# Graph attention and transformer on one core: side work placed by hand among the products, masks turned as pairs of bytes, merged preparation steps

## The chip, the cores and the metric

The kernel runs on one core of a Trainium2 chip. The metric is the device time of one execution in microseconds; of three runs the median is given. A profile of one execution shows what each engine does: TensorE (PE, with its weight loads PEld), VectorE (DVE), ScalarE (ACT), GpSimd (POOL), and SyncE (SP), from whose queue all DMAs are issued.

## What is computed

Two graph attention layers run one after the other on the same 4096 x 4096 adjacency matrix of int32, and a transformer layer follows. There are 8 heads of 32 features.

```python
def _gat_layer(x, adj_mat, W, a):
    Wh = jnp.einsum('nd,hdo->hno', x, W)
    src = jnp.einsum('hno,ho->hn', Wh, a[:, :O])
    dst = jnp.einsum('hno,ho->hn', Wh, a[:, O:])
    e = jax.nn.leaky_relu(src[:, :, None] + dst[:, None, :], LRELU_SLOPE)
    e = jnp.where(adj_mat[None, :, :] > 0, e, NEG_INF)
    alpha = jax.nn.softmax(e, axis=-1)
    out = jnp.einsum('hnm,hmo->hno', alpha, Wh)
    return jnp.transpose(out, (1, 0, 2)).reshape(N, -1)
...
h = jax.nn.elu(_gat_layer(x, adj_mat, W1, a1)) + x
out = jax.nn.elu(_gat_layer(h, adj_mat, W2, a2)) + h
...
qkv = layer_norm(x, g1, be1) @ w_qkv
scores = jnp.where(mask, jnp.einsum('nhd,mhd->hnm', q, k) * SCALE, -jnp.inf)
out = jnp.einsum('hnm,mhd->nhd', softmax(scores), v).reshape(n, DIM)
x = x + out @ w_proj + b_proj
x = x + jax.nn.gelu(layer_norm(x, g2, be2) @ w1 + b1) @ w2 + b2
```

## The kernel before, in words

**How a graph layer becomes products.** The leaky ReLU has two branches, and the exponential of a sum is a product of exponentials. So the weights of a row over its neighbours are a sum over those neighbours whose term passes a threshold (one branch) and over the others (the other branch). The threshold test depends on row and neighbour and gives a 0/1 byte; everything else is a factor of the row or of the neighbour. The layer is then a set of TensorE products whose stationary operand is a tile of 128 x 128 bytes of fp8 (the test ANDed with the mask, or the mask alone) and whose moving operand is `vst`, the neighbours' values multiplied by their exponentials, as two halves of fp16 that together carry an fp32 value.

**Tiling.** The rows are cut into blocks; `TILES` gives their sizes in tiles of 128 rows: 4, 4, 8, 8, 8 for the first layer and 8, 8, 8, 8 for the second. A *group* is one layer, one block, one pair of heads `p` (4 of them) and four key tiles `g` (8 of them). The main loop runs over all groups in that order. A group of an 8-tile block has 8 x 4 x 4 = 128 products, written at L1234 into six PSUM banks that stay open over the eight groups of a head pair. At the end of a pair, ACT copies the banks out (L1240, L1246), and `pair_end` puts four steps (load, sum, divide, out) on the list `later`, one of which is taken per group.

**What lies beside the products.**
- `compare` (L1008) makes the bytes for the group two ahead: four key tiles of two heads, on DVE (L1023) or ACT (L1021), and then one AND with the mask on DVE (L1026). It needs `s_b`, a row of terms spread over the partitions by DMA (`s_fetch`, L1000).
- Masks: `mask_loads` brings 128 rows x 1024 columns of the adjacency as int32 (512 KB); `mask_turn` clips them to bf16 (DVE, L844), turns them with eight transposes (TensorE, L849) into a bank of the pool "turn" (two buffers), and ACT copies the bank to fp8 (L850). Block 0 keeps its masks in SBUF; the others are written to DRAM and fetched again by `mask_fetch` when their block comes. There are 128 such units, all in the first layer. The table `turns` tells which units go beside which group; units of block 0 go beside the first head pair.
- Preparation of four key tiles (`features`, `term_rows`, `values`): rows of x are loaded and turned (fp32 transposes L916, copies L919); the terms' rows are a product with 8 output rows (L926), copied (L934) and written to DRAM; values and terms of each tile are two double products of 272 columns (L942), followed by the sign change (L950), the exponentials (ACT, L953, L961), the check reduction (L954), two scales (L962), the product (L963), the fp16 half (ACT, L971) and the rest (DVE, L972). Eight preparations make a layer.

**What sets the order.** Inside the graph layers the instructions of each engine are ordered by the tile framework's own scheduler. The preparations of both layers start only when their layer starts: three ahead of its first product, the rest in the gaps between the tiles of the first five groups. In the attention part, TensorE, ACT and DVE follow the order of the program (`manual_schedule`); SP works its queue in the order that it is given.

**The transformer.** For each of eight blocks of 512 rows: normalisation, queries and keys in two fp16 halves written to DRAM and stacked back (`stack`, L1387), values kept. Then attention over 512 units, and then the projection and feed-forward part. Before the first unit of attention the queries of block 0 and its first four mask chunks are loaded (`load_queries`, `load_chunk`, L1467); pools for these are opened after the QKV part has closed its own.

## Time and profile before

| | |
|---|---|
| median of 3 runs | 3524.44 us (3523.82 to 3525.63) |
| profiled execution | 3524.0 us, mean granted TensorE clock 0.982 |
| busy: TensorE | 3357.4 us |
| busy: DVE | 2903.2 us |
| busy: ACT | 2730.9 us |
| busy: GpSimd | 1239.1 us, none of it between 51 and 1783 us |
| last product of the graph layers | 1783.6 us |
| first product of attention | 1914.3 us |
| last product of attention | about 3226 us |

Busy times are averages over stages with different limits, so a reading begins by cutting the span where the order of work changes. In a table of stretches each row gives the stretch, its length, and for each engine the busy time and, in brackets, the count of instructions; then the mean granted TensorE clock, the busy share of the DMA engines and their rate. In a row of groups by line, the first number after the bar is the busy time of all instructions of that line, the second the mean of one in nanoseconds, and after the second bar stands the idle time of the engine just before them with what ended it. In a row of waits the three numbers are the total in microseconds, the number of waits and the longest.

### The profile page before, as it was taken

Reading aid. Unit: us, or ns where it says so; the run is one execution under the profiler, and the core shown is the slowest. Engines: PE = TensorE matmul, PEld = TensorE weight load, DVE = VectorE, ACT = ScalarE, POOL = GpSimd, SP = SyncE. Lnnn points to the kernel's source line nnn. Section 1 sums busy time; section 2 is a strip of 40 time slices with the busy share of each in tenths; the row PEclk is TensorE's granted clock in tenths of the full one; section 3 lists DMA queues with packets and bytes.
Section 4 is the critical chain, followed back from the end, with each engine's and each line's share of the span. In section 5 each row is a group of like instructions: output and inputs, shape, how many; then the busy total and the mean of one; then the engine's idle time right before and its main releaser. Section 6 shows DMA issues by size and latency. Waiting matters only on the chain.

```text
span 3524.0 us, 99099 instructions
## 1 busy us (share of the span) xinstructions
PE 3357.4 (95%) x43715; PEld 2128.8 (60%) x43715; DVE 2903.2 (82%) x3580; ACT 2730.9 (77%) x3528; POOL 1239.1 (35%) x538
## 2 busy tenths in 40 slices
PE   6898999999989999999987999999999999997998
PEld 4698999999969999999963111111111121112666
DVE  5898999999889999999944999999999999996111
ACT  4799999998778888888854777777777777775332
POOL 0000000000000000000001999999999999996110
PEclk8999999999999999999998999999999999998999
DMA  4357554441221312111156010101010110002110
GB/s 140 123 191 242 167 167 157 157 123 39 68 62 33 86 39 80 45 58 37 26 135 171 10 40 13 37 19 31 25 25 25 25 37 13 28 9 68 44 47 25
DMA packets 199560, 252.76 MB, mean 72 GB/s; under 512 B 88080, under 2 KB 134672, under 8 KB 199120
## 3 DMA queue, kind: packets, MB, share of 16 engines
q1 hardware_dynamic: 199120, 246.34, 23.3%
q8 instruction: 344, 5.64, 0.7%
q14 instruction: 96, 0.79, 0.1%
HBM read 203.83 MB, written 42.47 MB: 70 GB/s over the span
## 4 chain that ended last, share of the span: by engine, by line
PE 73%; DVE 11%; ACT 9%; DMA 3%; issue 2%; POOL 2%; SPq 0%; DVEq 0%; ACTq 0%; POOLq 0%
PE bank L1234 34%; PE u_ps L1480 12%; PE u_av L1494 11%; PE u_dn L1494 6%; ACT t L1021 5%; DVE u_e L1489 4%; PE misc L1666 3%; PE misc L1419 2%; POOL u_both L1580 2%; DVE t L1023 1%; ACT u_ps L1487 1%; ACT stage L850 1%; DVE t L1026 1%; PE misc L1650 1%; PE turn L926 1%
## 5 line engine op out<-in xcount | busy, mean ns | idle before, releaser
L1234 PE MATMUL bank<-vst,t 128*128 128x66 f16 (+1 forms) x24576 | 1517.9, 203 | 22.0 <-DVE t L1026 15.5
L1234 PEld LDWEIGHTS <-t 128*128 128x128 fp8e4 x24576 | 1505.6, 97 | 33.2 <-DVE t L1026 18.0
L1234 PE MATMUL bank<-vst,mask 128*128 128x132 f16 x8192 | 1503.5, 222 | 0.0
L1021 ACT ACTIVATE t<-s_b,g_negd 128x1024 int8<-128x1024 f32 (+1 forms) x1296 | 1260.0, 1063 | 88.8 <-PE bank L1234 88.1
L1489 DVE SCALAR_TENSOR_TENSOR u_e<-u_mask,u_ps 128x1024 f32<-128x1024 uint8 x1024 | 1201.7, 1215 | 100.7 <-ACT u_ps L1487 95.8
L1580 POOL TENSOR_TENSOR u_both<-u_e 128x1024 f32<-128x1024 f32 x512 | 1199.8, 2367 | 238.5 <-DVE u_e L1489 238.3
L1487 ACT ACTIVATE u_ps<-u_ps 128x1024 f32<-128x1024 f32 x1024 | 1010.8, 1008 | 296.2 <-PE u_ps L1480 277.2
L1234 PEld LDWEIGHTS <-mask 128*128 128x128 fp8e4 x8192 | 803.6, 98 | 1.9 <-issue 0.9
L1026 DVE TENSOR_TENSOR t<-t,mask 128x2048 int32<-128x2048 int32 (+1 forms) x288 | 590.6, 2051 | 119.5 <-ACT t L1021 109.8
L1023 DVE TENSOR_SCALAR t<-s_b,g_negd 128x1024 fp8e4<-128x1024 f32 (+1 forms) x1008 | 638.5, 687 | 2.7 <-PE bank L1234 2.3
masks.py:197 POOL MEMSET u_ident<- 128x128 f32 x1 | 0.2, 204 | 1785.7 <-DMA u_wq<-in_L_gnn_w_qkv_dram 1785.7
L1480 PE MATMUL u_ps<-u_q,u_k 128*128 128x512 f16 x2048 | 580.5, 384 | 36.8 <-DMA u_q<-half_d 21.7
L1480 PEld LDWEIGHTS <-u_k 128*128 128x128 f16 x2048 | 139.2, 97 | 743.7 <-issue 685.4
L1494 PE MATMUL u_av<-u_e,u_v 128*32 128x512 f32 x4096 | 547.1, 605 | 0.0
L1494 PE MATMUL u_dn<-u_both,u_ones 128*32 128x512 f32 x2048 | 274.0, 605 | 1.3 <-POOL u_both L1580 1.3
L1494 PEld LDWEIGHTS u_av<-u_e,u_v 128*32 128x32 f32 x4096 | 80.9, 108 | 219.1 <-issue 211.3
L1657 ACT ACTIVATE u_hid<-misc,u_b 128x512 f32<-128x512 f32 x64 | 42.3, 683 | 142.9 <-PE misc L1650 142.8
L850 ACT ACTIVATE stage<-turn 128x1024 fp8e4<-128x1024 bf16 x112 | 114.2, 1037 | 1.1 <-PE turn L849 1.0
L1673 DVE TENSOR_TENSOR u_xres<-u_xres,misc 128x256 f32<-128x256 f32 x32 | 13.5, 421 | 122.7 <-PE misc L1666 122.7
L1666 PE MATMUL misc<-u_w,u_hid 128*128 128x256 f32 x512 | 111.8, 379 | 0.0
L1650 PE MATMUL misc<-ln_cols,u_w 128*128 128x512 f32 x256 | 111.2, 592 | 0.0
L1494 PEld LDWEIGHTS u_dn<-u_both,u_ones 128*32 128x32 f32 x2048 | 40.6, 108 | 110.9 <-issue 108.4
(104 smaller groups left out, 1749.8 us busy)
## 6 DMA issues: line engine op xcount, KB each, us to landing
g_rows<-in_adj_dram SPq DMA_DIRECT2D x128, 512.0 KB
mask<-mask SPq DMA_DIRECT2D x120, 256.0 KB
s_b<-s_d SPq DMA_DIRECT2D x56, 512.0 KB
u_mask<-mask SPq DMA_DIRECT2D x32, 512.0 KB
mask<-stage SPq DMA_DIRECT2D x28, 512.0 KB
half_d<-u_halves SPq DMA_DIRECT2D x32, 256.0 KB
u_k<-half_d SPq DMA_DIRECT2D x32, 256.0 KB
u_q<-half_d SPq DMA_DIRECT2D x32, 256.0 KB
```

Of the source, the lines that this page charges most:

```text
L850: nc.scalar.activation(staged[0].rearrange("p i g n -> p (i g) n")[:, :, t * P : (t + 1) * P], pt, AF.Identity, saturate=False,)
L1021: nc.scalar.activation(to.bitcast(I8), s, AF.Sign, bias=negd, scale=-1.0)
L1023: nc.vector.tensor_scalar(to, s, negd, None, op0=ALU.is_ge, saturate=False)
L1026: nc.vector.tensor_tensor(both, both, mask.unsqueeze(1).to_broadcast(list(both.shape)), op=ALU.bitwise_and)
L1234: nc.tensor.matmul(to, left, right, start=k not in opened, stop=last)
L1480: nc.tensor.matmul(ps[:, j, :], k_st[:, h, mt * P : (mt + 1) * P], q_st[:, h, :], start=True, stop=True,)
L1487: nc.scalar.activation(ps, ps, AF.Exp, scale=SCALE)
L1489: nc.vector.scalar_tensor_tensor(e, mask, 0.0, ps, op0=ALU.not_equal, op1=ALU.mult)
L1494: nc.tensor.matmul(to[j * O : (j + 1) * O, :], lefts[j], es[j // 2][:, j % 2, :], start=start, stop=stop,)
L1580: nc.gpsimd.tensor_tensor(both, es_of[i - 1][u], es_of[i][u], op=ALU.add)
L1650: nc.tensor.matmul(ph, w1_sb[:, k, f * P : (f + 1) * P], hn[:, k, :], start=(k == 0), stop=(k == DC - 1),)
L1666: nc.tensor.matmul(po[:, :D], hid[:, f, at : at + P], w2_sb[:, f, :], start=(f == 0), stop=(f == FC - 1),)
```

## The change

1. **Blocks**: `TILES` of the first layer becomes 8, 8, 8, 8, so all groups have 128 products.
2. **Masks**: a unit is now 256 rows x 512 columns. `mask_clip` clips to fp8, with the bytes of two neighbouring rows side by side; the pair is read as one fp16 element, so `mask_turn` needs four transposes, and ACT copies 512 elements of 16 bits. Clips are placed one or two groups ahead of their transposes. A check at the start tests that four bit patterns survive a transpose.
3. **Preparation**: the weights carry a third set of 8 columns (the destination term times the slope), the sign, slope and the factor 32 are multiplied into the weights, so one exponential of 16 columns replaces two of 8; one copy takes both sets of terms; the fp16 rest is subtracted on GpSimd (`split`), a step later. The terms' rows come from one transpose of a 128 x 32 tile of the terms kept in SBUF, in place of the product with 8 output rows, and four small DMAs write them. The call of `check_values` is gone.
4. **Order**: TensorE, ACT and DVE follow the program's order in the whole of the graph layers. For each group a list `side` of steps with positions between 0 and 1 is made (preparation, compare, AND, mask turns, clips, pair-end steps), sorted, and given out between the tiles of the group's products.
5. **Change of layer**: the weights of the second layer are made during the first; six of its eight preparations stand beside the last six groups of the first layer, and two beside its own groups 3 and 4.
6. **QKV and attention**: the pools of queries and masks are opened before QKV; key stacks are issued one block later; the queries of block 0 and its four mask chunks are loaded during QKV. Normalisation pools are split (`u_ln`, `u_lnc`), the halves get three buffers.
7. **Feed-forward**: the projection weight's load is issued first, and two pools change places.

```diff
-TILES = ((4, 4, 8, 8, 8), (8, 8, 8, 8))
+TILES = ((8, 8, 8, 8), (8, 8, 8, 8))
...
-    mask_p = ctx.enter_context(tc.tile_pool(name="g_mask", bufs=11))
+    mask_p = ctx.enter_context(tc.tile_pool(name="g_mask", bufs=10))
...
+    def mask_clip(nb, c, i):
+
+        v = rows_p.tile([P, G * P, 2], F8, name="adj_8", bufs=6)
         nc.vector.tensor_scalar(
-            v.rearrange("p m s -> p (m s)"), r, 1.0, -(2.0**-30), op0=ALU.min, op1=ALU.max
-        )
...
+            v.rearrange("p m r -> p r m"),
+            loaded.pop((nb, c, i)),
+            1.0,
+            -(2.0**-30),
+            op0=ALU.min,
+            op1=ALU.max,
             saturate=False,
         )
+        clipped[nb, c, i] = v.rearrange("p m r -> p (m r)").bitcast(F16)
+        load_ahead(1)
...
+        pt = turn_bank([P, G, P], F16)
+        for m in range(G):
+            nc.tensor.transpose(pt[:, m, :], v[:, m * P : (m + 1) * P], ident_h)
+        to = built[nb, c][:, i // 2].bitcast(U16)
+        nc.scalar.activation(to[:, :, i % 2 * P : (i % 2 + 1) * P], pt.bitcast(U16), AF.Copy)
...
-        nc.vector.tensor_tensor(halves[:, :, 1, :], part, halves[:, :, 0, :], op=ALU.subtract)
+        def split(t):
+            part = held.pop(t).rearrange("p h i v -> p h (i v)")
+            halves = vst[q][:, t].rearrange("p h (k v) -> p h k v", k=2)
+            nc.scalar.copy(halves[:, :, 0, :], part)
+            nc.gpsimd.tensor_tensor(halves[:, :, 1, :], part, halves[:, :, 0, :], op=ALU.subtract)
...
+        def term_rows():
+
+            pr = bank()[: G * H, :P]
+            nc.tensor.transpose(
+                pr, L.terms[:, 0, G * q : G * (q + 1)].rearrange("p t h -> p (t h)"), ident_f
+            )
+            sr = some.tile([G * H, P], F32, name="g_sr")
+            nc.scalar.copy(sr, pr)
+            for t in range(G):
+                at = (G * q + t) * P
+                nc.sync.dma_start(s_d[l][:, at : at + P], sr[t * H : (t + 1) * H])
...
+    prepared = {i: (0, i + 2) for i in range(NG - 2)}
+    for l in range(1, NL):
+        start = l * len(TILES[0]) * per_block
+        for q in range(NG):
+            prepared[start + q + (-6 if q < NG - 2 else -3)] = (l, q)
...
+    ordered = {mybir.EngineType.PE, mybir.EngineType.Activation, mybir.EngineType.DVE}
+    ctx.enter_context(tc.manual_schedule(engines=ordered))
+    begin()
...
+        if made:
+            steps = preparation(*made, lambda: turn_bank([P, 512], F32))
+            beside(steps, 0.0, 0.9)
+        if i + 2 < len(groups):
+            steps = compare(i + 2)
+            beside(steps[:-1], 0.25 if made else 0.0, 0.95)
+            beside(steps[-1:], 0.96, 1.0)
+        beside([lambda u=u: mask_turn(*u) for u in turns.get(i, ())], 0.0, 0.9)
...
+            while side and (n == tiles - 1 or side[0][0] * tiles < n + 1):
+                side.pop(0)[1]()
...
-                    if i == 1:
-                        stack(k_st[:, :, cols], 1, (0, 0, 1, 1), cols)
...
+                for b in (nb - 1,) if nb + 1 < NNB else (nb - 1, nb):
+                    if b >= 0:
+                        at = slice(b * NB, (b + 1) * NB)
+                        stack(k_st[:, :, at], 1, (0, 0, 1, 1), at)
+                    if b == 0:
+                        load_queries(0)
+                if 2 <= nb < 2 + NT // MC:
+                    load_chunk(0, nb - 2)
```

## Prediction

> **What bounds the kernel now.** I read first the busy shares (TensorE 95% of the span), then cut the span where the order of the work changes and asked for the busy time of each engine in each stretch:
>
> ```profile
> core 0: us, PE busy (x) PEld busy (x) DVE busy (x) ACT busy (x) POOL busy (x), PEclk, DMA share, GB/s
> 0.00:51.20 51.20, 22.98 (x98) 13.10 (x98) 29.22 (x83) 23.12 (x55) 1.08 (x8) 0.92 0.54 156
> 51.20:155.50 104.30, 84.15 (x784) 60.58 (x785) 74.91 (x201) 67.25 (x166) 0.00 (x0) 0.88 0.37 118
> 155.50:368.60 213.10, 193.65 (x3973) 189.39 (x3971) 197.51 (x390) 210.64 (x342) 0.00 (x0) 0.98 0.65 211
> 368.60:961.30 592.70, 590.25 (x12786) 587.66 (x12787) 536.73 (x643) 546.31 (x648) 0.00 (x0) 1.00 0.39 122
> 961.30:1076.00 114.70, 101.93 (x1120) 74.28 (x1119) 103.94 (x249) 84.68 (x197) 0.00 (x0) 0.97 0.22 66
> 1076.00:1783.60 707.60, 707.57 (x15493) 705.70 (x15490) 637.49 (x734) 618.64 (x740) 0.00 (x0) 1.00 0.17 49
> 1783.60:1914.30 130.70, 94.16 (x322) 57.14 (x322) 49.41 (x103) 63.01 (x159) 0.61 (x2) 0.86 0.72 181
> ```
>
> The sixth stretch is the floor: 121 groups of 128 products (a group is four key tiles of one head pair in a block of 8 tiles) in 707.6 us, 5.85 us each, TensorE never idle; there DVE is busy 5.27 us and ACT 5.11 us a group. The graph layers hold 256 such groups, 1497 us, but end at 1783.6. The other 287 us lie in the other five stretches: 51 us before the first product; 81 over the floor in the first head pair of block 0 (512 products, 23.4 us worth); 50 in the rest of the two 4-tile blocks, where ACT is full (210.6 of 213.1); 31 in the blocks of 8 whose masks are turned beside them; 74 at the change of layer. A second look, at the waits between QKV and attention, shows one more hole, in which TensorE, then ACT and DVE behind it, wait for a load:
>
> ```profile
> PE u_ps L1480 <- DMA u_q<-half_d: 21.7, 1, 21.7
> ```
>
> Prices are from the groups by line:
>
> ```profile
> L850 ACT ACTIVATE stage<-turn 128x1024 fp8e4<-128x1024 bf16 x112 | 114.2, 1037 | 1.1 <-PE turn L849 1.0
> L844 DVE TENSOR_SCALAR adj_bf<-g_rows 128x1024 bf16<-128x1024 int32 x128 | 87.0, 685 | 3.6 <-DMA g_rows<-in_adj_dram 3.6
> L942 PE MATMUL turn<-g_w_ext,g_ft 128*128 128x272 f32 x256 | 71.9, 412 | 9.1 <-DVE g_prod L963 6.1 <-DVE g_negd L950 1.1 <-ACT g_rows L934 0.5
> L972 DVE TENSOR_TENSOR vst<-g_prod,vst 128x528 f16<-128x528 f32 x64 | 44.8, 700 | 0.5 <-ACT vst L971 0.3
> L963 DVE TENSOR_TENSOR g_prod<-turn,g_prod 128x512 f32<-128x512 f32 x64 | 43.9, 686 | 0.1
> L926 PE MATMUL turn<-g_ft,g_w_ext 128*8 128x512 f32 x64 | 37.0, 709 | 0.3 <-ACT g_ft L919 0.2
> ```
>
> The reader is to see 128 mask units of 1.04 us on ACT and 0.69 us on DVE, and a preparation that costs DVE more than TensorE.
>
> **What the Trainium skill says.** "Vector Engine (DVE) Microarchitecture Reference", section 5.1, lets a one-source operation with source and destination in SBUF and an even outermost dimension take two elements a cycle, whatever the type; two-tensor operations not. The trace agrees: the clip L844 takes 0.67 ns an element, the mask AND L1026 2.28 us for 2048. "TensorE: Matmul & The Clock Gate", Part 1, has 55.6 ns between products of 128 columns; here a group with eight transposes lasts 6.26 us against 5.84, 53 ns each. "SBUF — State Buffer", "Who interferes with whom": GpSimd shares a port pair with DVE's two-element mode and with the second input of DVE's two-tensor operations, and the later one waits out the whole instruction. No run here shows that: GpSimd is idle in the graph layers.
>
> **The change part by part.** All sums are against the profiled span, 3524.0 us (other runs 3523.8 to 3525.6).
>
> *Masks.* A unit keeps its 1024 elements a partition, but two rows become one 16-bit column: 4 transposes in place of 8, so TensorE 0.22 us in place of 0.44, and ACT copies 512 elements, priced as the 512-element copy L919, 0.59 us in place of 1.04. The DVE clip now writes single bytes two apart. If it keeps the two-element mode it stays at 0.64 us net (two in 1.29); if not, 1024 elements at the AND's 1.11 ns are 1.14 us. I take 0.64: the page's condition does not ask for step one. Both ends go into the range. Loads keep 512 KB, in pieces of 2 KB in place of 4; the 155.5 to 368.6 stretch moved 211 GB/s at 0.65 busy, and four loads plus writes in a 15 us group need some 190: I cost that at nothing, hidden behind DVE.
>
> *Blocks of 8 tiles throughout.* 64 half groups become 32 whole ones; the products stay 32,768. Comparing 1024 in place of 512 columns saves a fixed part only.
>
> *Preparation (16 times: 8 four-tile steps, two layers).* TensorE loses L926 (4 x 512 columns of fp32; 1.9 us in the timeline) for one small transpose, keeps 8 transposes (0.9) and 8 double-pass products, now 280 columns (3.8): 4.8 us in place of 6.6. DVE loses the subtraction L972 (to GpSimd) and one small scale, keeps copy, reduction, product, scale: 0.16 + 0.42 + 0.69 + 0.17, four times 1.44, less overlap 5.2 us. ACT loses one small exponential a tile and the 512-wide row copy. The end checks of a layer's values (L974) are no longer called: a few small reductions, hidden under TensorE, 0. GpSimd gets 528 elements a tile; by L1580 (2.37 us for 1024) an estimate of 1.2 us. Port waits cost DVE between 0 and 4.8 us a preparation; I take 2.0 in the first, 1.5 in the second layer.
>
> *Start.* Only layer 0's weights are made (DVE free near 11.5 us in place of 13.7), two preparations with eight clips take 2 x 7.8 + 5 for filling and ports (32), term rows to DRAM and back as before 6.5 (39), four compares on ACT and the AND 6.5: first product near 47. The second group's compare and four more clips follow on DVE: 5 carried over. 52.
>
> *Groups 0 to 5*, each with a preparation and four units. DVE: compares 2.3, AND 2.2, preparation 5.2, clips 2.6, ports 2.0 = 14.3; ACT 12.6; TensorE 5.85 + 4.8 + 0.9 = 11.5. Before, DVE-bound groups at the change of layer held DVE 91% busy; I take 15.2. Six are 91.
> *Groups 6 to 27*, 1.45 units each: TensorE 6.17, DVE 5.27 + 0.93 = 6.20, ACT 5.97. I take 6.25: 138.
> *Groups 28 to 91*, one unit each: TensorE 6.07, DVE 5.91, ACT 5.70. 64 x 6.08 = 389.
> *Groups 92 to 121*: 30 x 5.85 = 176.
> *Change of layer.* Six preparations beside groups 122 to 127, two beside 131 and 132. DVE 2.3 + 2.2 + 5.2 + 0.8 + 1.5 = 12.0, TensorE 10.65; I take 12.6: 76; then 3 x 6.3 + 2 x 12.6 = 44. The rows of the last block must be written by the last pair end, two steps a group, before step 6 reads them one group ahead: covered by a group of 6 us.
> *Groups 133 to 255*: 123 x 5.85 = 720.
> Sum 52 + 91 + 138 + 389 + 176 + 76 + 44 + 720 = 1686 against 1783.6: **-98**.
>
> *QKV and attention.* Queries and masks of block 0 are loaded inside QKV (3 MB more in about 100 us at 0.72 busy; TensorE has work there throughout), key stacks one block late, so SP no longer waits at each. Attention can start once the last banks are emptied, about 1895 in place of 1914.3; I take -17 of at most -20 and at least -10, since work buffers reuse space under the last stores. *Pools and the projection weight's earlier load*: the 11.9 us wait there is for the attention output, not the weight; 0, bounds -5 and +3. The pair end in fixed order delays the first normalisation of QKV by some 2 us: +1.
>
> Total 3524 - 98 - 17 + 1 = **3410**.
>
> **The rivals.**
> *A, as summed*: 3410, own range 3390 to 3430. Chance 0.55.
> *B, the byte-strided clip loses the two-element mode*: +0.5 us on 128 clips, on the path where DVE binds: start 4, six groups x 2.0 = 12, 22 x 0.65 = 14, 64 x 0.28 = 18, sum +48: 3458. For it: its two halves now interleave byte by byte in the destination. Against: the page. 0.20.
> *C, preparation groups bound by the exchange between three engines over two PSUM banks*, not by DVE: before, groups 2 and 4 of the first pair took 21.2 and 21.7 us. At +4 us on 14 groups: 3466. Against: those groups also waited for loads and an unplanned order. 0.12.
> *D, slower*: the fixed order hands a wait to every group. DVE has 0.58 us to spare in 5.85; an AND that waits for ACT costs 1.86 us (29 times, 53.9 us, in the sixth stretch, harmless there). If two of three groups wait so on the path, (1.24 - 0.58) x 250 = +165: 3575. It decides for slower from about 1.05 us a group. Against: the AND is two groups ahead of its products. 0.07.
> *E, less change than thought*: byte pairs not preserved, so that the general layers run, or gains lost elsewhere by chance, within 0.2%: 0.03. Better than A's range: 0.03.
>
> **How the numbers follow.** The likeliest is A, 3410. The range takes A's lower bounds (ports free: 6 x 2.0 + 8 x 1.5 = -24, rounded to -30 with the start) to C: 3380 to 3470. About 0.2% (7 us) is what a measurement can tell from no change. A, B, C and the better end are faster by more; D slower: 0.90, 0.03, 0.07.
>
> **What would show it.** L844's successor at 0.69 or 1.14 us; mask copies at 0.59; groups 28 to 91 at 6.1 us; groups 0 to 5 near 15 with DVE full, near 11.5 if ports cost nothing; no gap at the layer change; no 21.7 us wait for queries. A steady group above 5.9 us, or a first product after 60 us, would make the forecast wrong.

## The result, and the profile after

The changed kernel takes **3542.8 us** (median of 4 executions, 3537.5 to 3543.3) against 3524.8 us before: ratio 1.0048, 95% interval 1.003 to 1.0065. It is slower by half a per cent, where 3410 us had been forecast. The profiled execution is the shortest of the four, with a span of 3535.7 us; the sums below are made against it.

The stretches of the kernel after, cut at the steps of the forecast (start, groups 0 to 5, 6 to 27, 28 to 91, 92 to 121, 122 to 132, 133 to 255), show where the time is:

```profile
core 0: us, PE busy (x) PEld busy (x) DVE busy (x) ACT busy (x) POOL busy (x), PEclk, DMA share, GB/s
0.00:71.57 71.57, 23.77 (x84) 15.45 (x85) 25.33 (x74) 21.41 (x47) 10.28 (x16) 0.68 0.54 165
71.57:166.30 94.73, 77.35 (x1014) 65.67 (x1015) 82.86 (x152) 66.55 (x142) 31.45 (x23) 0.97 0.64 199
166.30:314.06 147.76, 137.09 (x2948) 135.61 (x2946) 136.20 (x165) 129.00 (x171) 2.19 (x2) 1.00 0.60 191
314.06:739.00 424.94, 396.67 (x8448) 393.37 (x8448) 387.47 (x470) 362.99 (x457) 0.00 (x0) 0.98 0.48 148
739.00:921.20 182.20, 176.39 (x3840) 174.90 (x3841) 160.76 (x180) 157.71 (x190) 0.00 (x0) 1.00 0.18 50
921.20:1054.40 133.20, 111.58 (x1613) 98.83 (x1611) 109.73 (x203) 89.47 (x182) 37.95 (x31) 0.96 0.27 83
1054.40:1807.00 752.60, 724.03 (x15748) 717.13 (x15745) 656.07 (x745) 629.61 (x750) 1.82 (x2) 1.00 0.17 50
```

The last stretch is 123 groups at 6.12 us. Before, TensorE was never idle in such a stretch and a group took 5.85 us; now it is idle for 29 of 753 us, though DVE is idle for 97 of them and ACT for 123. No engine is full: the engines wait for one another. The fourth stretch loses 28 us in the same way, and in the first DVE works 25 of 71.6 us. The graph layers end at 1807.0 us in place of 1783.6.

Who waits for whom stands in the groups by line. The rows of before (product after a compare, AND, the pair end's exponential):

```profile
L1234 PE MATMUL bank<-vst,t 128*128 128x66 f16 (+1 forms) x24576 | 1517.9, 203 | 22.0 <-DVE t L1026 15.5 <-ACT ev_narrow L1246 6.3
L1026 DVE TENSOR_TENSOR t<-t,mask 128x2048 int32<-128x2048 int32 (+1 forms) x288 | 590.6, 2051 | 119.5 <-ACT t L1021 109.8 <-ACT mask L850 2.3
L1079 ACT ACTIVATE e_ex<-e_z 128x512 f32<-128x512 f32 (+1 forms) x36 | 21.1, 585 | 33.1 <-DVE e_z L1075 33.0
```

and the same three after:

```profile
L1297 PE MATMUL bank<-vst,t 128*128 128x66 f16 (+1 forms) x24576 | 1528.4, 203 | 95.9 <-DVE t L1072 93.4 <-ACT ev_narrow L1309 1.4
L1072 DVE TENSOR_TENSOR t<-t,mask 128x2048 int32<-128x2048 int32 x256 | 588.7, 2300 | 166.5 <-ACT t L1065 147.9 <-DVE t L1067 0.5
L1127 ACT ACTIVATE ev_broad<-ev_broad 128x512 f32<-128x512 f32 x32 | 20.7, 646 | 175.3 <-DVE ev_broad L1124 175.3
```

Read from the bottom: ACT stands idle 175 us before 32 exponentials of 0.65 us, 5.5 us each time, waiting for DVE's division. Its compares, queued behind, come late, so DVE waits 148 us for them before its AND, and TensorE waits 93 us for the AND.

A part of one head pair on the timeline of DVE after, in the last stretch (start and duration in us; in brackets the idle time ahead of it and what ended it):

```profile
1425.64 1.25 DVE L1100 TENSOR_TENSOR ev_broad<-ev_broad 128x1056 f32<-128x1056 f32 x1
...
1428.83 0.43 DVE L1115 TENSOR_TENSOR ev_broad<-ev_broad,ev_narrow 128x264 f32<-128x264 f32 x1
1429.18 0.75 DVE L1067 TENSOR_SCALAR t<-s_b,g_terms 128x1024 fp8e4<-128x1024 f32 x1
1430.02 2.29 DVE L1072 TENSOR_TENSOR t<-t,mask 128x2048 int32<-128x2048 int32 x1
...
1434.11 0.69 DVE L1124 TENSOR_TENSOR ev_broad<-ev_broad,e_inv 128x512 f32<-128x512 f32 x1
1434.72 1.41 DVE L1067 TENSOR_SCALAR t<-s_b,g_terms 128x1024 fp8e4<-128x1024 f32 x2
1437.65 2.29 DVE L1072 TENSOR_TENSOR t<-t,mask 128x2048 int32<-128x2048 int32 x1 [1.52 <-ACT t L1065]
```

the timeline of ACT in the same place:

```profile
1418.79 10.54 ACT L1065 ACTIVATE t<-s_b,g_terms 128x1024 int8<-128x1024 f32 x10
1434.89 0.65 ACT L1127 ACTIVATE ev_broad<-ev_broad 128x512 f32<-128x512 f32 x1 [5.56 <-DVE ev_broad L1124]
1435.44 15.69 ACT L1065 ACTIVATE t<-s_b,g_terms 128x1024 int8<-128x1024 f32 x15
```

and that of TensorE:

```profile
1440.00 0.29 PE L1297 MATMUL bank<-vst,t 128*128 128x132 f16 x3 [1.64 <-DVE t L1072]
```

The sum of the pair end (six operations, 1425.64 to 1429.26) lies in one piece on DVE and puts DVE 3.6 us behind. ACT, which has run ahead of it, reaches the exponential, which the fixed order has put directly behind the division, and stops for 5.56 us. From there it works without a pause for at least 15.7 us, and the AND at 1437.65 still had to wait for it. That AND ends at 1439.94, and the group's products start 0.06 us later: nothing is left of the lead, the time from the end of an AND to the first product that uses it.

Before, the scheduler had let the pair end go by in small pieces; ACT's timeline there shows the same exponential with a wait of 1.36 us, and after it waits for TensorE to free a buffer, so ACT was as far ahead as the buffers allow:

```profile
1422.51 0.63 ACT L1079 ACTIVATE e_ex<-e_z 128x512 f32<-128x512 f32 x1 [1.36 <-DVE e_z L1075]
1423.05 9.45 ACT L1021 ACTIVATE t<-s_b,g_negd 128x1024 int8<-128x1024 f32 x9
1432.85 4.27 ACT L1021 ACTIVATE t<-s_b,g_negd 128x1024 int8<-128x1024 f32 x4 [0.36 <-PE bank L1234]
```

Outside the graph layers the u_q wait of 21.7 us is gone, but QKV takes 114.8 us from its first transpose to attention in place of 117.9 with that wait in it, 96.2 without. The waits of TensorE's transposes for DVE's normalised rows, before and after:

```profile
PE misc L1365 <- DVE ln_rows L1349: 1.3, 1, 1.3
PE misc L1425 <- DVE ln_rows L1409: 24.0, 5, 8.6
```

The longest of the five, 8.6 us, lies ahead of the first transpose; the other four, 15.4 us, lie inside the 114.8.

Behind the first product of attention the kernel is 4.4 us shorter than before (1605.3 against 1609.7 us). So the graph layers lose 23.4 us, QKV and the rest win 7.3 and 4.4: the 11.7 us between the two profiled executions.

### The profile page after: what moved, and what is told of

The parts are those of the page before. It is cut to its first block, busy times and chain, and to the rows that moved or that the text cites. A ratio compares the mean times of both kernels' runs of the same rounds, so it can differ in the third digit from the quotient of the medians.

```text
span 3535.7 us, 97670 instructions
## 1 busy us (share of the span) xinstructions
PE 3303.7 (93%) x43156; PEld 2100.3 (59%) x43156; DVE 2883.3 (82%) x3265; ACT 2641.9 (75%) x3318; POOL 1323.7 (37%) x602
## 4 chain that ended last, share of the span: by engine, by line
PE 38%; DVE 7%; ACT 4%; POOL 2%; issue 1%; DMA 1%; SPq 0%; DVEq 0%; ACTq 0%; POOLq 0%
PE u_ps L1549 12%; PE u_av L1563 11%; PE u_dn L1563 6%; DVE u_e L1558 4%; PE misc L1732 3%; PE bank L1297 2%; PE misc L1497 2%; POOL u_both L1646 1%; ACT u_ps L1556 1%; PE misc L1716 1%; DVE t L1072 1%; ACT t L1065 1%; PE misc L1516 1%; ACT ln_square L1401 1%; PE misc L1425 1%
## 5 line engine op out<-in xcount | busy, mean ns | idle before, releaser
L1065 ACT ACTIVATE t<-s_b,g_terms 128x1024 int8<-128x1024 f32 x1152 | 1238.9, 1163 | 38.0 <-PE bank L1297 29.3
L1072 DVE TENSOR_TENSOR t<-t,mask 128x2048 int32<-128x2048 int32 x256 | 588.7, 2300 | 166.5 <-ACT t L1065 147.9
L1067 DVE TENSOR_SCALAR t<-s_b,g_terms 128x1024 fp8e4<-128x1024 f32 x896 | 638.5, 756 | 9.0 <-DMA s_b<-s_d 9.0
L1006 POOL TENSOR_TENSOR vst<-g_prod,vst 128x528 f16<-128x528 f32 x64 | 82.6, 1292 | 972.8 <-ACT vst L1005 969.2
L1127 ACT ACTIVATE ev_broad<-ev_broad 128x512 f32<-128x512 f32 x32 | 20.7, 646 | 175.3 <-DVE ev_broad L1124 175.3
```

The source lines that it names most:

```text
L1006: nc.gpsimd.tensor_tensor(halves[:, :, 1, :], part, halves[:, :, 0, :], op=ALU.subtract)
L1065: nc.scalar.activation(to.bitcast(I8), s, AF.Sign, bias=negd, scale=-1.0)
L1067: nc.vector.tensor_scalar(to, s, negd, None, op0=ALU.is_ge, saturate=False)
L1072: nc.vector.tensor_tensor(both, both, m32.unsqueeze(1).to_broadcast(list(both.shape)), op=ALU.bitwise_and)
```

## The experiments

The theory T1 from the reading above: **the fixed order makes ACT stand behind DVE's division once per head pair**. The rivals: DVE's burst as such, or the place of compares and ANDs in every group; the start is a ring of waits of its own; QKV has its own cause.

### The exponential one step later

```diff
             nc.vector.tensor_tensor(
                 z, z, inv.unsqueeze(3).to_broadcast([P, n, 2, O]), op=ALU.mult
             )
-            nc.scalar.activation(held["ex"], z, AF.Exp)
             held["z"] = z
+        def step_exp():
+            nc.scalar.activation(held["ex"], held["z"], AF.Exp)
...
-        later.extend([step_load, step_sum, step_divide, step_out])
+        later.extend([step_load, step_sum, step_divide, step_exp, step_out])
...
-        beside([take] * (2 if l > 0 and nb == 0 and p == 0 else 1), 0.1, 1.0)
+        beside([take] * (3 if l > 0 and nb == 0 and p == 0 else 1), 0.1, 1.0)
```

> The changed kernel with one edit at the pair end: ACT's exponential (L1127) leaves the step of DVE's division (L1124) and comes one group later as a step of its own, five steps in place of four. Theory T1 (the fixed order makes ACT stand behind DVE's z, 175 us in all; compares and ANDs come late behind it and the products wait): ACT's wait before the exponential falls from 175 us to under 20, DVE's AND waits less than 80 us for ACT in place of 147.9, products wait less than 40 us for the AND in place of 93.4, a head pair of groups 133 to 255 goes from 49.0 back to 46.8 to 47.3 us, of groups 28 to 91 from 53.1 to about 49; total 3455 to 3475 us (65 to 85 below the changed kernel). Rival T2 (what delays is DVE's own burst of some 3.5 us in one group, or the AND that waits for the last compare of every group): the wait before the exponential goes too, but the products still wait 75 us or more; total 3520 us or more.

Measured: 3485.4 us (3483.8 to 3490.1), ratio to before 0.9892 (0.9876 to 0.9909); 57 us below the changed kernel by the medians. The three groups by line:

```profile
L1299 PE MATMUL bank<-vst,t 128*128 128x66 f16 (+1 forms) x24576 | 1522.2, 203 | 46.2 <-DVE t L1072 43.2 <-ACT ev_narrow L1311 1.1 <-issue 0.3
L1072 DVE TENSOR_TENSOR t<-t,mask 128x2048 int32<-128x2048 int32 x256 | 588.3, 2298 | 111.5 <-ACT t L1065 90.2 <-DVE t L1067 0.5
L1130 ACT ACTIVATE ev_broad<-ev_broad 128x512 f32<-128x512 f32 x32 | 20.6, 643 | 10.6 <-DVE ev_broad L1124 10.6
```

The wait before the exponential falls from 175 to 11 us, DVE's wait for ACT before the AND from 148 to 90, and TensorE's wait for the AND from 93 to 43 (T1 had under 80 and under 40 for these two). Groups 133 to 255 gain 26.7 us (725.9), groups 28 to 91 17.0 (408.0). So T1 holds for about half of the loss, and the time lies 10 us above T1's interval. What T1 left out is seen in the mean duration of a group by its place in the pair: the third group still lasts 7.2 us in groups 28 to 91, as it did with the wait; only the fourth and fifth became shorter (8.16 to 6.74, 7.08 to 6.06).

### The sum spread over three groups

On top of the last edit:

```diff
-        later.extend([step_load, step_sum, step_divide, step_exp, step_out])
+        later.extend(
+            [step_load, step_sum, step_over, step_scale, step_divide, step_exp, step_out]
+        )
...
-        beside([take] * (3 if l > 0 and nb == 0 and p == 0 else 1), 0.1, 1.0)
+        beside([take] * (4 if l > 0 and nb == 0 and p == 0 else 1), 0.1, 1.0)
```

(`step_sum` keeps the addition of the halves, `step_over` has the two subtractions, `step_scale` the scale and the two additions.)

> The kernel with the later exponential, and besides the pair end's sum (five operations of DVE, some 3.5 us in one group) cut into three steps in three groups. Theory T2' (what is left after the exponential moved is DVE's burst: the group behind it lasts 7.2 us in groups 28 to 91 where the scheduler's order has 6.05, and 6.1 to 6.2 us in two groups of a pair later on): groups 28 to 91 fall from 408 to 387 to 394 us, 133 to 255 from 726 to 716 to 720, ACT's part of the wait before the AND (90 us) falls under 60; total 3450 to 3462 us. Rival T3 (what is left is the place of compares and AND in every group): the two stretches stay over 402 and 723 us, total 3475 us or more.

Measured: 3466.5 us (3464.0 to 3467.0), ratio 0.983 (0.9813 to 0.9846), another 19 us by the medians. Groups 133 to 255 are at 716.1, the floor: each group 5.82 us. There exponential and burst were the whole cause. Groups 28 to 91 fell to 398.6 only, short of the 387 to 394 expected; ACT's part of the wait before the AND is 75 us, not under 60, and the total lies 4.5 us above what was expected. The row of groups 28 to 91 suggests why a fixed order has less room there:

```profile
303.50:702.10 398.60, 392.07 (x8451) 389.15 (x8449) 386.35 (x471) 363.08 (x458) 0.00 (x0) 1.00 0.52 159
```

DVE has 386 us of work in a stretch that TensorE can do in 387. The layer change became 6.9 us longer (137.3 against 130.3 us). There the pair end's seven steps must go by in two groups, which is the likely reason; no run isolates it.

### The graph layers in the scheduler's order

```diff
     ordered = {mybir.EngineType.PE, mybir.EngineType.Activation, mybir.EngineType.DVE}
-    ctx.enter_context(tc.manual_schedule(engines=ordered))
     begin()
```

> The changed kernel with its graph layers handed to the scheduler of the framework, as in the kernel before, in place of the fixed order; all else stays. If the fixed order as such is the cause (T1 and T2 alike), ACT's wait before the pair end's exponential falls to about the 33 us of before and the steady groups go back to 5.85 us: total 3430 to 3480 us. If the cause lies in what is computed (blocks of 8 tiles throughout, pairs of bytes, rows by small transposes), the steady groups of 133 to 255 stay at 6.1 us on the mean and the total at 3520 us or more. A third way: the scheduler spreads the pair end well and the preparations badly, so that groups 28 on gain 60 us and the first 30 groups lose as much.

Measured: **3418.2 us** (3412.8 to 3418.6), ratio 0.9698 (0.9681 to 0.9714), better than any of the three ways foreseen. Everything else of the change is in this kernel. Its stretches, cut at the same groups as those shown of the changed kernel:

```profile
0.00:62.86 62.86, 29.32 (x129) 20.12 (x130) 43.00 (x100) 29.09 (x66) 14.00 (x19) 0.85 0.71 218
62.86:139.50 76.64, 70.94 (x970) 60.81 (x971) 70.93 (x130) 60.13 (x123) 26.12 (x20) 0.97 0.77 242
139.50:277.20 137.70, 135.91 (x2948) 135.46 (x2946) 137.32 (x180) 129.71 (x172) 1.53 (x1) 1.00 0.65 201
277.20:664.20 387.00, 387.00 (x8453) 387.00 (x8450) 373.64 (x456) 359.55 (x457) 0.00 (x0) 1.00 0.52 160
...
964.30:1680.70 716.40, 716.30 (x15748) 715.95 (x15744) 640.32 (x741) 628.11 (x750) 1.39 (x2) 1.00 0.18 52
```

TensorE is never idle from group 28 to the layer change, nor after it. Two things differ from the fixed order in how the work lies. First, work is done earlier. In the start DVE works 43 us where the fixed order has 25: a third preparation, five more clips (14 against 9) and five more compares lie there. The 14 instructions of DVE that make the second layer's weights lie in groups 6 to 27 (180 instructions against 165) and no longer in groups 28 to 91 (456 against 470). Second, the AND keeps its lead: from the timelines, the first product of a group starts on the mean 1.76 to 4.66 us (by place in the pair) after its AND ended in groups 138 to 255, against 0.06 us in the fourth, fifth and sixth group of a pair in the changed kernel. ACT still waits 71 us in all before the exponential here, at most 2.6 us at a time, and in the whole of the graph layers TensorE waits 7.5 us for an AND, 5.7 of them before its first product. A wait costs nothing as long as it doesn't use up the lead that stands behind it.

### The start

```diff
             for k, step in enumerate(steps):
                 step()
                 if k in (3, 5, 7, 9):
-                    u = mine.pop(0)
-                    mask_clip(*u)
-                    mask_turn(*u)
+                    if turning:
+                        mask_turn(*turning.pop(0))
+                    mask_clip(*mine[0])
+                    turning.append(mine.pop(0))
+            mask_turn(*turning.pop(0))
```

> The changed kernel with one edit in begin(): each unit of the mask is clipped one step before it is turned, so that TensorE never turns a unit that DVE has only just been asked for. Theory S1 (the start is a ring: values, clip, turn, next values, 4.8 us a step): steps of about 2.5 to 3 us, first product at 56 to 61 us in place of 71.6, total 10 to 15 us below the changed kernel, groups 0 to 5 as they were (94.7). Rival S2 (the loads and the cold clock set the start): first product at 68 us or later, total within 4 us of the changed kernel.

Measured: 3535.1 us (3526.4 to 3536.1), ratio 1.0024 (1.0013 to 1.0036), 8 us below the changed kernel by the medians, with intervals of the two ratios that just overlap. First product at 62.2 us in place of 71.6, with groups 0 to 5 (94.1) and the later stretches as they were. Both the first product and the total fall short of S1's intervals (56 to 61 us; 10 to 15 us gained). The ring that this takes apart, on the timeline of the changed kernel:

```profile
28.50 0.69 DVE L864 TENSOR_SCALAR adj<-g_adj 128x1024 fp8e4<-128x1024 int32 x1
29.25 0.61 PE L886 MATMUL turn<-g_ident_h,adj 128*128 128x128 f16 x4 [2.35 <-DVE adj L864]
...
31.93 0.18 ACT L981 ACTIVATE g_big<-bank 128x16 f32<-128x16 f32 x1 [0.91 <-PE bank L972]
32.01 0.17 ACT L984 ACTIVATE g_r<-bank 128x8 f32<-128x8 f32 x1
32.22 0.17 DVE L985 COPY g_terms<-bank 128x16 f32<-128x16 f32 x1 [3.02 <-ACT g_r L984]
```

TensorE waits for the clip, DVE waits for the values that TensorE makes behind the turn, and the next clip stands behind that: 4.8 us from clip to clip (28.50 to 33.31), of which DVE works 1.8 us. The granted clock belongs to the picture: the same 84 instructions of TensorE in the start take 23.8 us at a mean granted clock of 0.68 in the changed kernel and 19.2 us at 0.80 with this edit. So about half of the 9 us is TensorE's own time, and a part of what S2 names is in it.

A second run for the start: `begin()` as it was, but ahead of the fixed order, so that the scheduler arranges it alone; with the two edits of the pair end and the third buffer of QKV (below).

```diff
-    ctx.enter_context(tc.manual_schedule(engines=ordered))
     begin()
+    ctx.enter_context(tc.manual_schedule(engines=ordered))
```

> The fixed order kept for the groups, with the later exponential, the spread sum and the third buffer for QKV's rows, but begin() itself, as it is written in the changed kernel, handed to the scheduler (the fixed order starts after it). It asks where the free order's 25 us up to the end of group 5 come from (164 us there with the fixed order, 139.5 with the free one). If they lie in the order within the start: first product at 50 to 58 us, groups 0 to 5 at 94, 144 to 152 us together, total 3428 to 3440 us. If they come from work of the first groups that the scheduler pulls into the start's idle time, which this edit doesn't allow: first product at 58 to 64 us, groups 0 to 5 at 94, total 3440 to 3450 us, as with the clip one step ahead (3446 us).

Measured: 3439.5 us (3438.3 to 3443.8), ratio 0.9767 (0.9751 to 0.9784). First product at 56.6 us, groups 0 to 5 in 92.3: 148.9 us together, against 164.2 with the fixed start and the same groups, and 139.5 in the free order. So some 15 of the 25 us are the order within the start, as the first of the two expectations had it. For the other 9 the likely cause is the work of later groups that only the free order does in the start, the third preparation above all; no run isolates it.

### QKV

```diff
-            some = qkv.enter_context(tc.tile_pool(name="u_qkv", bufs=2))
+            some = qkv.enter_context(tc.tile_pool(name="u_qkv", bufs=3))
```

> The changed kernel with a third buffer for the rows of QKV, so that the scheduler, which orders this stage, puts a block's mean two blocks ahead and not behind the previous block's split. Theory Q1 (QKV is 18 us longer than before, 114 against 96.5, because three blocks of transposes wait 3.9 us each for a normalisation that DVE began too late and then run at half clock): QKV falls to 96 to 100 us, the three waits of 3.9 us are gone, total 12 to 18 us below the changed kernel. Rival Q2 (the loads of keys, queries and masks that were moved into the stage slow it): QKV stays over 108 us, total within 5 us of the changed kernel.

Measured: 3532.4 us (3527.9 to 3536.5), ratio 1.0024 (1.0016 to 1.0031). QKV takes 107.2 us, and the total is 10 us lower by the medians, with intervals of the ratios that just overlap: between the two theories. Two of the three waits of 3.9 us before a block's transposes are gone, and the third, of the last block, has become longer:

```profile
1897.65 2.19 PE L1425 MATMUL misc<-u_ident,ln_rows 128*128 128x128 f32 x8 [7.33 <-DVE ln_rows L1409]
```

In this kernel the mean of that last block still stands behind 24 of the 32 subtractions with which DVE makes the fp16 halves, as without the edit; the others moved forward. The two waits that are left inside the stage, 3.7 and 7.3 us, are as long as what QKV still takes over 96.2 us (11.0). The late normalisation is a cause, then, and the buffer only a part of its cure; that the moved loads cost nothing isn't shown, and that the change gave the normalisation's pool two buffers in place of three wasn't tried.

The opposite choice for both stages: free graph layers, and QKV in the order in which it is written, with the third buffer.

```diff
+            qkv.enter_context(
+                tc.manual_schedule(
+                    engines={
+                        mybir.EngineType.PE, mybir.EngineType.Activation, mybir.EngineType.DVE
+                    }
+                )
+            )
             standing = {nb: ready(nb) for nb in range(2)}
```

> The opposite for the two stages: the graph layers handed to the scheduler as in the run of the free order (3418 us), and QKV, which the scheduler ordered so far, in the order in which it is written (a block's normalisation two blocks ahead of its use), with the third buffer for its rows. If the late normalisation is what lengthens QKV: no wait of TensorE for DVE's ln_rows after the first block, QKV 96 to 100 us in place of 115, total 3398 to 3405 us, and this is the version to keep. If a fixed order costs a stage its engines' slack whatever the stage: QKV 110 us or more, total 3413 us or more.

Measured: 3409.2 us (3408.3 to 3409.7), ratio 0.967 (0.9654 to 0.9686), again between the two expectations. QKV is at 107.3 us, no better than with the buffer alone. From the third block on no transpose waits for ln_rows, but the second block's still wait 5.0 us, and the value products of two later blocks wait 3.7 and 1.0 us for ACT; DVE, in the written order, had stopped twice for a load of rows, 16.8 us in all, which may be what held ACT up. What would bring QKV back to 96 us stays open.

### The split on DVE

The free order, with the subtraction on DVE as it was before the change:

```diff
-            nc.gpsimd.tensor_tensor(halves[:, :, 1, :], part, halves[:, :, 0, :], op=ALU.subtract)
+            nc.vector.tensor_tensor(halves[:, :, 1, :], part, halves[:, :, 0, :], op=ALU.subtract)
```

> The run of the free order with one edit: the subtraction of the split (64 times) on DVE, as in the kernel before, and not on GpSimd. P1 (GpSimd's work beside DVE costs DVE next to nothing, so the move was worth its full 64 x 0.70 us where DVE is the bound): groups 0 to 5 go from 76.6 to 88 to 93 us, the layer change from 125.5 to 130 to 134, total 3438 to 3450 us. P2 (the prediction's price: DVE loses 2.0 and 1.5 us a preparation to port waits, so most of the gain is given back): groups 0 to 5 rise by 5 us or less, total 3421 to 3430 us.

Measured: 3409.4 us (3407.6 to 3410.2), ratio 0.9669 (0.9652 to 0.9685): both expectations fall, since the kernel is not slower but 9 us faster by the medians, though the intervals of the two ratios just overlap. The graph layers end 7.0 us earlier in the profiled executions (1673.7 against 1680.7): the change of layer takes 117.7 us in place of 125.5; groups 0 to 27 end at the same time (277.6 and 277.2), though by another way: the start and groups 0 to 5 are 12 us shorter together (127.3 against 139.5) and groups 6 to 27 13 us longer (150.3 against 137.7). Where DVE's saving went shows in the groups of the free order, with the subtraction on GpSimd,

```profile
L1006 POOL TENSOR_TENSOR vst<-g_prod,vst 128x528 f16<-128x528 f32 x64 | 90.7, 1420 | 875.1 <-ACT vst L1005 851.7 <-ACT g_big L981 21.7 <-PE bank L1296 1.7
L1000 DVE TENSOR_SCALAR g_prod<-g_big 128x16 f32<-128x16 f32 x64 | 31.8, 497 | 14.0 <-ACT g_r L984 7.6 <-ACT g_big L981 5.1 <-POOL vst L1006 1.3
```

and on DVE:

```profile
L1006 DVE TENSOR_TENSOR vst<-g_prod,vst 128x528 f16<-128x528 f32 x64 | 44.3, 703 | 0.4 <-ACT vst L1005 0.2
L1000 DVE TENSOR_SCALAR g_prod<-g_big 128x16 f32<-128x16 f32 x64 | 11.2, 174 | 13.9 <-ACT g_big L981 13.9
```

A scale of 16 elements lasts 497 ns on the mean beside GpSimd and 174 without it. That gives back 20.6 of the 44.3 us that the move took from DVE; the subtraction itself takes 1.42 us on GpSimd in place of 0.70.

The same edit with the fixed order kept:

> The changed kernel, fixed order and all, with one edit: the subtraction of the split on DVE and not on GpSimd. In the free order this edit gained 8 us at the change of layer and nothing before it. If what counts there is the length of the chain (GpSimd 1.29 us against DVE 0.70 us) and the port, which are the same in both orders: groups 0 to 5 at 88 to 94 us, groups 122 to 132 at 122 to 132 in place of 133, total 3528 to 3540 us. If in the fixed order the 0.70 us a tile have no room, since every instruction of DVE keeps its place in front of a compare: groups 0 to 5 at 97 to 108 us, total 3548 to 3570 us.

Measured: 3537.7 us (3535.7 to 3538.6), ratio 1.0047 (1.0031 to 1.0062), as the changed kernel within 0.2%: the first of the two expectations. Groups 0 to 5 take 94.1 us (94.7 with GpSimd), the change of layer 129.8 (133.2). The row of groups 0 to 5:

```profile
71.52:165.62 94.10, 76.14 (x1015) 64.71 (x1015) 86.11 (x174) 66.53 (x142) 0.00 (x0) 0.98 0.62 200
```

The compares in it, with GpSimd's subtraction (the changed kernel) and without it (this run):

```profile
L1067 DVE TENSOR_SCALAR t<-s_b,g_terms 128x1024 fp8e4<-128x1024 f32 x24 | 24.6, 1043 | 0.0
L1067 DVE TENSOR_SCALAR t<-s_b,g_terms 128x1024 fp8e4<-128x1024 f32 x24 | 17.7, 746 | 0.0
```

DVE has 22 more instructions than in the changed kernel (174 against 152), 15.5 us of work at 0.70 each, but is busy only 3.3 us longer (86.1 against 82.9). Most of the other 12.2 us is what its instructions lose beside GpSimd: by their durations 7.1 us in the compares, 2.8 in the clips and 0.7 in the scales, 1.8 us in each of the six preparations.

### The versions put together

All repairs with the fixed order kept: exponential, spread sum, clip ahead, third buffer.

> All repairs together, with the fixed order kept: exponential later, sum spread, the start's clip one step ahead of its turn, third buffer for the rows of QKV. If they are separate causes the gains add: first product at 61 to 63 us, groups 0 to 5 at 94, 28 to 91 at 387 to 394, 133 to 255 at 716 to 720, QKV at 107, total 3432 to 3446 us, and what remains to the free order's 3418 lies in the first 28 groups (17 us in groups 0 to 5, 5 in 6 to 27). If the free order's gain rests on something else than these places, the total stays over 3460 us.

Measured: 3446.1 us (3444.7 to 3449.6), ratio 0.9773 (0.9756 to 0.9789): at the upper end of what was expected. First product at 61.4 us, groups 133 to 255 at 716.1, QKV at 108.3: the repairs add up (by the medians the two of the pair end gained 76 us, the other two 8 and 10; all together 97). What remains to the free order does not lie in the first 28 groups alone, as was expected: groups 0 to 5 take 95.8 us against 76.6, but groups 28 to 91 stay at 398.6 against 387.0 and the change of layer takes 138.6 against 125.5.

Free graph layers, split on DVE, QKV as written with the third buffer:

> The two versions at 3409 us put together: graph layers in the scheduler's order, the split's subtraction on DVE, QKV in the order in which it is written with a third buffer for its rows. If the two gains over the free order (8 to 9 us each by the medians, from different stages: layer change and QKV) are real and separate: 3397 to 3404 us. If one of them is chance between executions: 3407 to 3412 us.

Measured: **3398.6 us** (3397.0 to 3402.5, 5 executions), ratio 0.9653 (0.964 to 0.9666). This is what was expected if the two gains are real and separate. By the ratios it lies about 0.0016 below each of the two versions, with intervals that overlap. It beats both kernels, the one before by 3.5% and the changed one by about 4%.

## Why the prediction was wrong

The durations in us by the steps of the forecast, from the profiled executions:

| stretch | forecast | changed kernel | exponential later | and sum spread | free order |
|---|---|---|---|---|---|
| start | 52 | 71.6 | 70.1 | 70.1 | 62.9 |
| groups 0 to 5 | 91 | 94.7 | 93.9 | 94.1 | 76.6 |
| 6 to 27 | 138 | 147.8 | 143.0 | 139.3 | 137.7 |
| 28 to 91 | 389 | 424.9 | 408.0 | 398.6 | 387.0 |
| 92 to 121 | 176 | 182.2 | 176.5 | 174.6 | 174.6 |
| 122 to 132 | 120 | 133.2 | 130.3 | 137.3 | 125.5 |
| 133 to 255 | 720 | 752.6 | 725.9 | 716.1 | 716.4 |
| end of the graph layers | 1686 | 1807.0 | 1747.7 | 1730.2 | 1680.7 |

**What failed is the step from work to time.** Each sum of the form "64 x 6.08" or "123 x 5.85" took the busy time of the fullest engine as the duration of the group. With the same work in the scheduler's order, the end comes at 1680.7 us where 1686 had been summed; the fixed order doesn't reach that, by 126 us. From group 6 on each term is met in that order to within 6 us. Ahead of it, luck is in the sum: the start took 11 us more and groups 0 to 5 14 us less than forecast, since one of the six preparations lay in the start. The page of before couldn't show that, since it had the pair end spread by the scheduler; the written order could: step_divide has an operation of ACT directly behind an operation of DVE, and step_sum has six operations of DVE in one place. The forecast priced these lines as averages.

**Rival D named the mechanism, and was given 0.07 for a wrong reason.** It had an AND that waits for ACT in the fixed order, and against it: "the AND is two groups ahead of its products". It is written two groups ahead, but at the end of that group's list; in the changed kernel it ended between 0.06 and 3.05 us before its products, by place in the pair. The lead to hold a wait against was 3 us or less, not two groups of 5.85. D's place was wrong too: it had two of three groups wait, for 165 us; the groups without a lead are the three of eight behind the pair end's division.

**Groups 133 to 255 (720, measured 752.6).** Shown: exponential 26.7 us, sum 9.8.

**Groups 28 to 91 (389, measured 424.9).** Exponential 17.0, sum 9.4; of the 11.6 that remain to the free order only this is shown, that DVE's work (386 us) nearly fills the stretch, while the scheduler had the second layer's weights, 14 instructions of DVE, made earlier. The forecast's 5.91 us of DVE a group measured 6.05. A part of the 17.0 is the clock: in the changed kernel it was granted at 0.5 in four stretches of 3.4 us, with the later exponential in one, in the free order in none. The estimate for the three fewer, 3 x 3.4 x 0.5, is 5 us.

**Start (52, measured 71.6).** "Two preparations with eight clips take 2 x 7.8 + 5" is DVE's work again. (The forecast's own steps add up to 45 us, not to the 47 that it gives for the first product.) In the fixed order the clip and its turn form a ring of 4.8 us a step; a step's distance between the two gained 9 us, the scheduler's order of the start about 14 (70.1 to 56.6), in both cases with a higher granted clock than the changed kernel's 0.68 (0.80 and 0.84).

**Groups 0 to 5 (91, measured 94.7)** came near for another reason than the one given. DVE was put at 14.3 of 15.2 us a group; it was busy for 82.9 of the 94.7 us, and with the subtraction back on it (3.3 us more busy in all) the six groups took no longer, 94.1. So DVE wasn't full in this order, and the time that it gained stayed unused. The price of the port waits came near: 1.8 us a preparation where 2.0 was taken, and 1.4 at the change of layer (11.2 us in eight) where 1.5 was.

**Change of layer (120, measured 133.2).** In the free order 125.5, with the split on DVE 117.7. In the fixed order with both edits of the pair end it takes 137 to 139 us, 12 to 13 more than in the free order, and these are not explained; the order of the groups with a preparation wasn't tried.

**QKV and attention (-17, measured -7).** From the end of the graph layers to attention, 123.4 us in place of 130.7. The u_q wait went as forecast. But the sum took for granted that QKV's own work would stay where it was; it took 114.8 us where 96.2 had been net of that wait. The third buffer took back 7.6 us of it, and the 11.0 that are left there are as long as the waits for the last normalisations; what would remove them is open.

**Right:** the clip with bytes two apart keeps the mode of two elements (715 ns in the changed kernel, 695 where GpSimd is idle, against 685 before; rival B had 1.14 us). So rival B fell, and the page that was set against it, "Vector Engine (DVE) Microarchitecture Reference", section 5.1, which asks nothing of the step for that mode, agrees with the trace. The turned masks' copy on ACT was put at 0.59 us and took 0.60 to 0.62, GpSimd's subtraction at 1.2 us and took 1.29. Rival C, preparation groups bound by the exchange between the engines, is not what the free order shows: there groups 0 to 5 took 12.8 us each, with five of the six preparations in them and DVE busy for 93%. In the fixed order no engine was full in them, and how much of that is C's exchange over two banks isn't shown.

## What to carry to other kernels

A group's duration is the fullest engine's busy time only if no engine runs out of lead; in a fixed order, put beside each busy time the lead of each hand-over (start of the user minus end of the maker) and hold every in-order wait and every burst against it. Don't put an instruction of one engine directly behind its maker on another where the two engines drift apart: a step of distance cost nothing here and gained 57 us. And before trusting a hand-written order, run the same work in the scheduler's: the difference is the price of the order, here 125 of the 133 us by which the forecast failed.

## What the runs showed of the hardware

GpSimd's subtraction makes instructions of DVE wait, and the means over a whole kernel hide which. In the free order the compares took 753 ns on the mean beside GpSimd's subtraction and 748 without it, the AND 2294 and 2288, and only the scale of 16 elements stood out, with 497 and 174. The traces show more when DVE's instructions are sorted by whether a subtraction of GpSimd was already running when they began:

| DVE, mean ns | changed kernel: elsewhere | changed kernel: began inside one | free order: elsewhere | free order: began inside one |
|---|---|---|---|---|
| scale L1000, 16 elements | 171 | 782 (14 of 64) | 178 | 642 (44 of 64) |
| compare L1067, 1024 elements | 748 | 1092 (23 of 896) | 747 | 1009 (20 of 896) |
| clip L864, 1024 elements | 693 | 1259 (5 of 128) | 692 | 871 (7 of 128) |
| AND L1072, 2048 elements | 2292 | 2758 (4 of 256) | 2288 | 2586 (5 of 256) |
| reduction L988, input in PSUM | 412 | 414 (13 of 56) | 412 | 411 (16 of 56) |

One such pair in the free order:

```profile
29.79 1.15 POOL L1006 TENSOR_TENSOR vst<-g_prod,vst 128x528 f16<-128x528 f32 x1 [0.78 <-ACT g_big L981]
29.97 1.01 DVE L1000 TENSOR_SCALAR g_prod<-g_big 128x16 f32<-128x16 f32 x1
```

The scale begins 0.18 us behind the subtraction and ends 0.04 us behind it. In all 72 instructions of these four kinds that lost over 0.1 us in the two traces, the end less the usual duration lies 0.13 to 0.20 us ahead of the subtraction's end. An instruction of DVE that had begun first lost nothing (21 compares of the changed kernel: 745 ns). So the later one waits for nearly the whole of the other, which is what "SBUF — State Buffer", "Who interferes with whom", says of GpSimd and DVE's two-element mode or two inputs in SBUF; reductions, and the product L994 with its one input from PSUM (679 ns in the free order, inside a subtraction and elsewhere), lost nothing. Which instruction pays depends on the order: in the free order mostly the scale, in the fixed order the compare as much. In all it is 21 us in the changed kernel and 28 in the free order, of the 44 us that the move took from DVE. Moving 0.70 us a tile to an engine that needs 1.3 to 1.4 us for it gained nothing in either order.
